# Leaf results of the last tree scattered to token order, in a Macaron block with hard-routed trees

## The chip, the cores and the metric

The kernel runs on one core of a Trainium2 chip. The metric is the device time of one execution in microseconds (us): the median of three runs. Engines are named as the profile names them: PE (TensorE; PEld its weight loads), DVE (VectorE), ACT (ScalarE), POOL (GpSimd) and SP (SyncE, which here only issues transfers).

## The reference, cut to what matters

```python
def fff(x, nw, nb, w1, b1, w2, b2, act):       # a tree of depth 8 with 256 leaves
    node = 0
    for _ in range(8):                          # hard routing, one leaf per token
        node = 2 * node + 1 + (x . nw[node] + nb[node] > 0)
    leaf = node - 255
    h = act(x @ w1[leaf] + b1[leaf])            # 256 -> 16
    return h @ w2[leaf] + b2[leaf]              # 16 -> 256

def ffn(x):
    xn = (x - mean(x)) / sqrt(std(x) + 1e-5)
    q, k, v = fff(xn, q.., relu), fff(xn, k.., relu), fff(xn, v.., relu)
    y = xn + softmax(q k^T / sqrt(256)) v       # one head, 1024 x 1024 per batch
    return y + fff(y, f.., gelu)

x = x + 0.5 * ffn(layernorm(x))
x = x + attention(layernorm(x))   # 16 heads of 16, latent k and v, RoPE, mask causal by pages of 64
x = x + 0.5 * ffn(layernorm(x))
```

x is 4 x 1024 x 256 in float32: 4096 tokens. The two FFNs have the same weights. The layer norm inside an FFN and its own norm are merged into one scale per token.

## The kernel before, in words

**Tiling.** Tokens go in 32 tiles of 128 (NT; a token's row lies on one partition), in groups of 4 tiles (GT), 8 tiles to a batch (TPB). `xres` holds the residual stream in SBUF, `xn` the normed rows, later y, with a column for the leaf number on either side.

**A tree** has five steps. *Route* (`route`, L293): transposes, matmuls with all node weights, comparisons (`bits`, L319), one-hot leaves (`hot`, L332). *Place* (`place`, L438, with `counts`, `ranks`): the 256 leaves are 32 blocks of 8; tokens are sorted by block into groups of 128 slots, each group of one block, so that a group may end in pads. *Scatter* (`scatter`, L506): POOL sends each tile's rows (257 wide, with the leaf number) to their slots in a DRAM buffer `xs`, one indirect DMA per tile. *Leaves* (`leaves`, L590): for each group an `xg` load, transposes (`xgT`), matmul with the block's w1 (`w_..`, turned by `load_first`, L543, from `raw_..` loads), a mask that keeps the token's own leaf (`hm`, L630), transposition with the activation (`hid`), matmul with w2, and the result row `og`, written to a DRAM buffer `os_..` in slot order. 48 groups are fixed; up to 15 more stand in branches (`spare_leaves`), of which the second FFN runs 5 for q and f. *Fetch* (`fetch`, L664, `fetch_b2`, L676): for each tile a POOL gather of the 128 result rows by slot, and one of the b2 rows by leaf, 128 KB each.

Pads must hold no stray leaf number, so `clear` (L240) writes zeros into both `xs` buffers (8.3 MB each) and into the spare parts of `os_q`, `os_k` and `os_v` (2.0 MB each), once, at the head of the first FFN. The clear of `xs[0]` is issued on SP, the rest on ACT.

**An FFN** runs: routes q; building w1 of q; scatter q; routes k beside it; leaves q; routes v; leaves k; leaves v, with gathers for the attention of batch 0; then the attention over 32 query tiles. Each tile has `score` (two matmuls with a width of 512 and a depth of 256 in two parts, maximum `mx` on DVE, exponential `pr` on ACT) and `weigh` (8 transposes, 8 matmuls with `vb`, row `xn` on DVE); one tile is scored ahead of the one weighed. In between stand the gathers of the next batch and the routing of f, four tiles after their last `weigh`. Tree f is placed in two runs: `place_early` for the first 24 tiles during the last batch's attention, with their 24 scatters, and `place_late` for the last 8 after the last `weigh`. Then come 8 scatters, the leaves of f, and in them `settle`, which gathers b2 of f for all tiles and adds y and b2, by halves, to `xres` (L1002). After the last leaf, 32 gathers `y_f` (L668) and 32 additions (L1012) close the FFN; the first FFN takes the moments of each row there, the second writes each tile out.

**Between the FFNs** stands the 16-head attention (MLA below), whose score matmuls (L1155, L1189) fill PE; its first tiles need all moments (`rstd`, L1097).

**The order.** A scheduler orders the instructions of each engine from the program's order and its own estimates; each engine, and each issuing queue, then runs strictly in that order. A tile buffer comes free when its last reader is done, so the number of buffers (`bufs`) sets how far loads run ahead.

Of the kernel before, what the change touches and what calls it, by code (L numbers as in the profile page):

```python
# [24 lines left out]
P = 128  # L25
# [46 lines left out]
def macaron_kernel(ctx: ExitStack, tc: tile.TileContext, a: dict, out: bass.AP):  # L72
# [33 lines left out]
    def sm(shape):  # L106
        return bank("sm", shape)
# [121 lines left out]
    xs = [dram.tile([NSLOT, XW], F32, name=f"xs_{n}") for n in range(2)] * 2  # L229
    osrt = [dram.tile([NSLOT, E], F32, name=f"os_{nm}") for nm in FFFS[:3]]  # L230
    osrt.append(osrt[0])
# [5 lines left out]
    zero = const.tile([P, XW], F32, name="zero")  # L237
    nc.vector.memset(zero, 0.0)
# [42 lines left out]

    def x_of(t):
        return xn[:, t, 1 : 1 + E]

    def row_of(f, t):
        lo = 1 - f % 2
        return xn[:, t, lo : lo + XW]
# [5 lines left out]
    def route(pool, f, t, oh, acc, leaf):  # L293
# [3 lines left out]
        xT = pool.tile([P, KC, GTOK], F32, name="xT", tag="xT")  # L297
        for i in range(0, GT, 2):
            pt = sm([P, KC, 2 * P])
            for k in range(2):  # L300
                for c in range(KC):
                    nc.tensor.transpose(  # L302
                        pt[:, c, k * P : (k + 1) * P], x_of(t + i + k)[:, c * P : (c + 1) * P], ident
                    )
            nc.scalar.copy(xT[:, :, i * P : (i + 2) * P], pt)  # L305
        yield
        bits = pool.tile([P, 2, GTOK], BF16, name="bits", tag="bits")
        for r in range(2):
            pl = sm([P, GTOK])
# [11 lines left out]
        hot = pool.tile([P, 2, GTOK], BF16, name="hot", tag="hot")  # L321
        for lc in range(2):
            ps = sm([P, GTOK])
# [10 lines left out]
        pr = sm([P, GT, NBLK + 2])  # L334
        for i in range(GT):
# [8 lines left out]
        nc.vector.tensor_copy(oh[:, t : t + GT, :], pr[:, :, :NBLK])  # L344
        for i in range(t, t + GT):
            nc.vector.tensor_tensor(acc[:, i + 1], acc[:, i], oh[:, i], ALU.add)
        nc.vector.tensor_copy(leaf[:, t : t + GT], pr[:, :, NBLK])
        lc = leaf_col(f)
        nc.vector.tensor_copy(xn[:, t : t + GT, lc : lc + 1], pr[:, :, NBLK + 1 :])
# [41 lines left out]
    def ranks(pool, oh, acc, slot, lo, hi, first, second=None):  # L391
# [7 lines left out]
        if second:  # L399
            past = pool.tile([P, n, NBLK], F32, name="past", tag="past")  # L400
            nc.vector.tensor_tensor(past, pr, bc(second[0], 1, n), ALU.is_ge)
            nc.vector.tensor_tensor(past, past, bc(second[1], 1, n), ALU.mult)
            nc.vector.tensor_tensor(row, pr, past, ALU.add)
            nc.vector.tensor_tensor(row, row, bc(first, 1, n), ALU.add)
        else:
            nc.vector.tensor_tensor(row, pr, bc(first, 1, n), ALU.add)
# [47 lines left out]
    EARLY = NT - TPB  # L454

    def place_early(pool, oh, acc, slot):

        ng = tiles_of(pool, counts(pool, acc, EARLY), EARLY)
        end = ends_of(pool, "gend", ng, 0.0)
        first = first_row(pool, end, ng)  # L460
        full = pool.tile([P, NBLK], F32, name="full", tag="full")
        nc.vector.tensor_scalar_mul(full, ng, float(P))
        yield
        for lo in range(0, EARLY, NT // 2):
            ranks(pool, oh, acc, slot, lo, min(lo + NT // 2, EARLY), first)
            yield
        gb = pool.tile([P, GCOL], F32, name="gb", tag="gb")
        for h in range(2):
            ended(pool, gb, end, h)
            yield  # L470

        past = pool.tile([P, GCOL], F32, name="gb_past", tag="gb_past")
        nc.vector.tensor_scalar(
            past, cst[:, C_G : C_G + GCOL], end[:, NBLK - 1 :], -float(NBLK), ALU.is_ge, ALU.mult
        )
        nc.vector.tensor_add(gb, gb, past)
        return end, first, full, gb

    def place_late(pool, oh, acc, slot, gblk, sel, end, first, full, gb):


        cnt = counts(pool, acc, NT)
        nc.vector.tensor_sub(cnt, cnt, full)
        ng = tiles_of(pool, cnt, TPB)
        more = ends_of(pool, "gend2", ng, end[:, NBLK - 1 :])

        skip = pool.tile([P, NBLK], F32, name="skip", tag="skip")
        nc.vector.tensor_sub(skip, more, ng)
        nc.vector.tensor_scalar_mul(skip, skip, float(P))
        nc.vector.tensor_sub(skip, skip, first)  # L490
        nc.vector.tensor_sub(skip, skip, full)
        yield
        ranks(pool, oh, acc, slot, EARLY, NT, first, (full, skip))
        yield
        gb2 = pool.tile([P, GCOL], F32, name="gb2", tag="gb2")
        for h in range(2):
            ended(pool, gb2, more, h)
        nc.vector.tensor_add(gb, gb, gb2)
        tile_blocks(gb, more, gblk, sel)
# [43 lines left out]
    def load_first(pool, f, w1, b1p, b1, raws):  # L543


        nc.vector.tensor_copy(b1p, b1)
        for k in range(1, 3):
            for q in range(k, 3):
                one = slice(q * NBLK, (q + 1) * NBLK)
                nc.vector.tensor_sub(b1[one], b1[one], b1p[one])  # L550
                nc.vector.tensor_copy(b1p[one], b1[one])
        nb_half = P // EPB
        for k, (hf, c) in enumerate(PART):
# [4 lines left out]
            for l0 in range(0, LW, 4):  # L558
# [4 lines left out]
                if l0 % 8:  # L563
# [10 lines left out]
    def spare_leaves(*what):  # L574
# [4 lines left out]
            engines=[getattr(mybir.EngineType, e) for e in ("PE", "DVE", "Activation", "SP")],  # L579
# [10 lines left out]
    def leaves(pool, f, w1, w2, b1p, sel, gblk, func, lo=0, hi=SPARE[0]):  # L590
# [3 lines left out]
        blk = {}  # L594
# [791 lines left out]
```

## Time and profile before

| | us |
|---|---|
| median of three runs (lowest to highest) | 3035.63 (3020.66 to 3035.7) |
| the profiled execution | 3026.19 |
| its span | 3024.0 |
| PE busy | 2507.0 (83%) |
| DVE busy | 1508.0 (50%) |
| ACT busy | 1055.0 (35%) |
| POOL busy | 827.2 (27%) |
| first FFN: routes q end, leaves q start, leaves q end | 73.9, 182.2, 269.7 |
| first FFN: attention begins, last weighing, first masked group and last result of f | 541, 913.3, 974.2, 1058.6 |
| MLA's first large matmul | 1121.1 |
| second FFN: routes q end, leaves q start | 2029, 2086 |
| second FFN: attention begins, last weighing, first masked group and last result of f | 2440, 2814.2, 2864.4, 2971.8 |

The mean granted clock of PE was 0.911. DMA moved 309 MB at 102 GB/s over the span, unevenly: near nothing during the MLA, near its most at the head. An engine's busy share over the whole span says little here, since stages with full PE alternate with stages in which it waits; what counts is what each wait is for.

### The profile page before, as it was taken

How to read it: one execution, taken by the hardware profiler on the slowest of the kernel's cores; microseconds unless marked ns; L12 is line 12 of the kernel's file. 1: busy time of each engine (PE TensorE's matmuls, PEld its weight loads, DVE VectorE, ACT ScalarE, POOL GpSimd, SP SyncE). 2: the span in 40 equal slices, each digit the busy share in tenths (PEclk: the TensorE clock that was granted, in tenths of full speed). 3: DMA queues.
4: the chain of work that ended last, by engine and by line, in shares of the span. 5: the costliest groups of instructions: out<-in, count | busy, mean ns of one | idle time of the engine just before them, and what ended most of it. 6: DMA issues, size and time to landing. Idle time of an engine off the chain costs nothing. (4 is left out here: it accounts for less than half of the span.)

```text
span 3024.0 us, 42420 instructions
## 1 busy us (share of the span) xinstructions
PE 2507.0 (83%) x14320; PEld 1506.8 (50%) x14360; DVE 1508.0 (50%) x3993; ACT 1055.0 (35%) x2466; POOL 827.2 (27%) x941
## 2 busy tenths in 40 slices
PE   7398988589893929999999999988889968889492
PEld 3156567356662614444444344355656745566361
DVE  8353544233345456666666576376354533334552
ACT  3134334122221303555555555433334422222130
POOL 0430324644225052100101100005204454431514
PEclk9699889799996959999999999998989889999796
DMA  9936467322114520000000000034546842210454
GB/s 267 296 118 218 150 203 215 123 63 65 42 49 148 162 74 1 1 1 1 1 1 1 1 1 2 1 102 163 174 160 214 245 149 65 69 49 34 145 172 143
DMA packets 225217, 309.26 MB, mean 102 GB/s; under 512 B 28248, under 2 KB 196312, under 8 KB 220888
## 3 DMA queue, kind: packets, MB, share of 16 engines
q1 hardware_dynamic: 148352, 166.10, 17.7%
q0 software_dynamic: 36864, 100.84, 10.8%
q10 hardware_dynamic: 39768, 39.36, 4.3%
q8 instruction: 128, 2.10, 0.3%
q14 instruction: 105, 0.86, 0.1%
HBM read 193.54 MB, written 112.66 MB: 101 GB/s over the span
## 5 line engine op out<-in xcount | busy, mean ns | idle before, releaser
L1162 DVE TENSOR_REDUCE mxh<-big 128x1 f32<-128x512 f32 (+3 forms) x768 | 393.1, 552 | 221.7 <-PE big L1155 219.6
L1196 ACT ACTIVATE pTh<-big 128x512 f32<-128x512 f32 (+3 forms) x768 | 336.8, 491 | 332.5 <-PE big L1155 296.3
L1155 PE MATMUL big<-kTh,qTh 32*128 32x512 f32 (+3 forms) x1536 | 407.8, 534 | 3.2 <-ACT kTh L1137 1.6
L1189 PE MATMUL big<-qTh,kTh 32*128 32x512 f32 (+3 forms) x1536 | 351.9, 529 | 0.0
L722 PE MATMUL sm<-vb,pT 128*128 128x256 f32 x1024 | 259.2, 410 | 64.7 <-DVE mx L703 49.5
L311 PE MATMUL sm<-xT,nwT 128*128 128x512 f32 x512 | 243.5, 620 | 54.4 <-ACT xT L305 54.2
L630 DVE SCALAR_TENSOR_TENSOR hm<-eid,xg,sm 128x128 f32<-128x128 f32 x399 | 138.4, 347 | 299.1 <-PE sm L625 294.7
L639 ACT ACTIVATE hid<-sm 128x128 f32<-128x128 f32 x399 | 110.8, 278 | 491.2 <-PE sm L637 490.3
L722 PEld LDWEIGHTS sm<-vb,pT 128*128 128x128 f32 x1024 | 205.6, 206 | 140.5 <-DVE mx L703 50.3
L694 PE MATMUL two<-kT,qT 128*128 128x512 f32 x512 | 247.9, 608 | 1.3 <-ACTq L584 1.3
L604 PE MATMUL sm<-ident,xg 128*128 128x128 f32 x798 | 166.0, 292 | 60.9 <-DMA xg<-xs 60.9
L1189 PEld LDWEIGHTS big<-qTh,kTh 32*128 32x128 f32 x1536 | 117.6, 183 | 149.2 <-DVE mxh L1162 75.6
L319 DVE TENSOR_SCALAR bits<-sm,thr 128x512 bf16<-128x512 f32 x128 | 95.7, 749 | 184.1 <-PE sm L311 183.8
L311 PEld LDWEIGHTS sm<-xT,nwT 128*128 128x128 f32 x512 | 96.8, 198 | 167.3 <-issue 95.0
L606 DVE COPY xgT<-sm 128x256 f32<-128x256 f32 x399 | 166.9, 418 | 25.4 <-PE sm L604 23.7
L1155 PEld LDWEIGHTS big<-kTh,qTh 32*128 32x128 f32 x1536 | 151.8, 183 | 45.1 <-ACT pTh L1196 27.4
L1207 PE MATMUL sm<-pTh,vpad 128*32 128x512 f32 (+3 forms) x1536 | 166.7, 498 | 4.7 <-ACT pTh L1196 4.7
L646 ACT COPY og<-sm 128x256 f32<-128x256 f32 x399 | 148.6, 372 | 49.1 <-PE sm L644 19.7
L305 ACT COPY xT<-sm 128x512 f32<-128x512 f32 x128 | 69.3, 590 | 191.1 <-PE sm L302 190.9
L508 POOL DMA_INDIRECT xs<-xn,slot_v x64 | 63.4, 991 | 251.9 <-DVE slot_v L412 232.9
L694 PEld LDWEIGHTS two<-kT,qT 128*128 128x128 f32 x512 | 91.3, 195 | 73.7 <-issue 66.9
L508 POOL DMA_INDIRECT xs<-xn,slot_f x64 | 67.7, 1058 | 217.0 <-DVE slot_f L412 198.7
(294 smaller groups left out, 4367.0 us busy)
## 6 DMA issues: line engine op xcount, KB each, us to landing
xg<-xs SPq DMA_DIRECT2D x399, 128.5 KB
os_q<-og SPq DMA_DIRECT2D x202, 128.0 KB
os_v<-og SPq DMA_DIRECT2D x101, 128.0 KB
os_k<-og SPq DMA_DIRECT2D x96, 128.0 KB
raw_q<-in_q_w SPq DMA_DIRECT2D x8, 1024.0 KB
w_q<-in_q_w SPq DMA_DIRECT2D x2, 4096.0 KB
raw_k<-in_k_w SPq DMA_DIRECT2D x8, 1024.0 KB
w_k<-in_k_w ACTq DMA_DIRECT2D x2, 4096.0 KB
```

Source lines behind the costliest of these rows:

```text
L311: nc.tensor.matmul(pl, nwT[:, c, f, r * P : (r + 1) * P], xT[:, c, :], start=(c == 0), stop=(c == KC - 1),)
L604: nc.tensor.transpose(pa[:, c, :], xg[:, x0 + c * P : x0 + (c + 1) * P], ident)
L606: nc.vector.tensor_copy(xT, pa)
L630: nc.vector.scalar_tensor_tensor(hm, eid, xg[:, lf : lf + 1], ph, ALU.is_equal, ALU.mult)
L646: nc.scalar.copy(og, po)
L694: nc.tensor.matmul(ps[:, n0 : n0 + 512], qT[:, c, i * P : (i + 1) * P], kT[:, c, n0 : n0 + 512], start=(c == 0), stop=(c == KC - 1),)
L722: nc.tensor.matmul(po, pT[:, j, :], vb[:, j, :], start=(j == 0), stop=(j == TPB - 1))
L1155: nc.tensor.matmul(ps[:, :n], qT[r : r + HPAD, hg, i * P : (i + 1) * P], kT[r : r + HPAD, hg, n0 : n0 + n], start=True, stop=True,)
L1162: nc.vector.tensor_reduce(maxima(b, hg)[:, i, c, u : u + 1], ps[:, :n], AX.X, ALU.max)
L1189: nc.tensor.matmul(ps[:, off:], kT[r : r + HPAD, hg, j * P : (j + 1) * P], qT[r : r + HPAD, hg, qb * QN + off : (qb + 1) * QN], start=True ...
L1196: nc.scalar.activation(pT[:, u, off:], ps[:, off:], AF.Exp, scale=1.0 / math.sqrt(HD))
L1207: nc.tensor.matmul(acc[r : r + HPAD, off:], vpads[b % 2][:, j, 4 * hg + 2 * pair + u, :], pTs[pair][:, u, off:], start=(j == 0), stop=(j = ...
```

## The change

Five things change.

1. The results of f are scattered by token. A token column (the tile's first token plus the partition) travels with each row of f through a buffer of its own, `xs_f`, 258 wide; its pads hold a number of 4096 or more. In `leaves`, f copies the column to an integer tile `tok` (6 buffers) and POOL scatters `og` to `ytok`, a DRAM buffer in token order; the bounds check skips the pads. So `y_f` is read back as eight plain loads of four tiles (`arrive`). In the first FFN these and the moments are woven into the MLA's start, after a first part for batch 0; in the second they stand before eight writes of the output.
2. `settle` (b2 of f and y added to `xres`) moves into the attention for 28 tiles, two gathers in flight; the last four tiles remain in leaves f.
3. f is placed in three runs, tiles 0 to 23, 24 to 27 and 28 to 31; the last routing is of one tile, the one before of three. w1 of f is copied by ACT alone.
4. Four query tiles are scored before the first is weighed (two of them use buffers of the routing).
5. All clears go to SP, those of the `os` buffers each to a place of its own; `xs_f` is cleared in each FFN, after the loads of f's first weights are asked for.

In the changed program's order on SP in the first FFN: `xs[1]`'s clear, `raw_q` parts 3 and 4, `os_q`'s clear, six `xg` loads of q with a `raw_k` load among them, `os_k`'s clear, three `b_v` loads, `os_v`'s clear, a `raw_k` load, `xs_f`'s clear, the seventh `xg`.

```diff
-    xs = [dram.tile([NSLOT, XW], F32, name=f"xs_{n}") for n in range(2)] * 2
+    xs = [dram.tile([NSLOT, XW], F32, name=f"xs_{n}") for n in range(2)]
     osrt = [dram.tile([NSLOT, E], F32, name=f"os_{nm}") for nm in FFFS[:3]]
-    osrt.append(osrt[0])
+
+    xs += [xs[0], dram.tile([NSLOT, XW + 1], F32, name="xs_f")]
+    ytok = dram.tile([NTOK, E], F32, name="ytok")
...
-    zero = const.tile([P, XW], F32, name="zero")
-    nc.vector.memset(zero, 0.0)
+    zero = const.tile([P, XW + 1], F32, name="zero")
+    nc.vector.memset(zero[:, :XW], 0.0)
+    nc.vector.tensor_scalar_add(zero[:, XW:], pid, float(NTOK))
...
+    RUNS = (0, NT - TPB, NT - GT, NT)
...
+            if f == 3:
+                tok[g] = pool.tile([P, 1], I32, name="tok", tag="tok", bufs=6)
+                nc.vector.tensor_copy(tok[g], xg[:, XW:])
...
+            if f == 3:
+                nc.gpsimd.indirect_dma_start(
+                    out=places[g],
+                    out_offset=bass.IndirectOffsetOnAxis(ap=tok.pop(g), axis=0),
+                    in_=og,
+                    in_offset=None,
+                    bounds_check=NTOK - 1,
+                    oob_is_err=False,
+                )
+            else:
+                nc.sync.dma_start(osrt[f][g * P : (g + 1) * P, :], og)
...
-                            nc.vector.tensor_scalar_mul(zero, count, 0.0)
-                            clear(nc.scalar, xs[1])
-                            for o in osrt[:3]:
-                                clear(nc.scalar, o[SPARE[0] * P :])
...
+                        if first:
+                            for rows in (xs[1], osrt[0][SPARE[0] * P :]):
+                                clear(nc.sync, rows)
...
+                        if first:
+                            clear(nc.sync, osrt[1][SPARE[0] * P :])
...
+                    if first:
+                        clear(nc.sync, osrt[2][SPARE[0] * P :])
...
+            clear(nc.sync, xs[3])
...
+                def settle(t):
+
+                    b2 = fetch_b2(pf, 3, t, leaf[3], bufs=2)
+                    yield
+                    for add in (x_of(t), b2):
+                        nc.vector.scalar_tensor_tensor(
+                            xres[:, t, :], add, 0.5, xres[:, t, :], ALU.mult, ALU.add
+                        )
...
+                        to = rp.tile([P, T], F32, name="pr", tag="xT") if s in (2, 3) else None
+                        scored.append((s, vb, *score(ap, qT, kT, i, to)))
+                        if s == 0:
+                            drain(values)
                         if b or i > 1:
                             next(ahead, None)
-                        elif i:
-                            drain(values)
-                        if late:
-                            t, v, *pr = late
-                            weigh(ap, v, t, *pr)
-                            for path in paths:
-                                for _ in range(1 + (b == B - 1)):
-                                    next(path, None)
-                            if t % GT == GT - 1:
-                                paths.append(route(rp, 3, t - GT + 1, *hot_f, leaf[3]))
-                        late = now
+                        if b and i == 0:
+                            next(ahead, None)
+                        if s >= 3:
+                            while len(scored) > 1:
+                                use()
+                                if s == 3:
+                                    next(ahead, None)
...
+                        if s >= 12:
+                            for t in (s - 12,) if b < B - 1 else (2 * s - 36, 2 * s - 35):
+                                settling.append(settle(t))
+                                next(settling[-1])
+                                if len(settling) > 2:
+                                    drain(settling.pop(0))
...
-                build = load_first(raw, 3, w1, b1p[3], b1, raws)
+                build = load_first(raw, 3, w1, raws, False)
                 w2 = load_second(nc.scalar, wp, 3)
-                for _ in route(rp, 3, t - GT + 1, *hot_f, leaf[3]):
+                for _ in paths[-1]:
                     drain(islice(build, 1))
-                late = place_late(pf, *hot_f, slot[3], gblk[3], sel[3], *placed)
+                late = placing(2)
                 next(late)
-                drain(islice(build, 3))
+                drain(islice(build, 4))
                 next(late)
-                scatter(3, slot[3], views, EARLY)
-                drain(late, build)
+                scatter(3, slot[3], views, RUNS[2])
+                drain(build, late)
+                split_b1(b1p[3], b1)
...
-                what = lp, 3, w1, w2, b1p[3], sel[3], gblk[3], AF.Gelu
-                with_steps(leaves(*what), settle())
+                what = lp, 3, w1, w2, b1p[3], sel[3], gblk[3], AF.Gelu, dram_disjoint_views(ytok, NGRP)
+                steps = leaves(*what)
+                drain(islice(steps, 8))
+                with_steps(steps, *[settle(t) for t in range(NT - GT, NT)])
                 spare_leaves(*what)
-                for t in range(NT):
-                    y = fetch(ep, 3, t, slot[3], bufs=4)
-                    nc.vector.scalar_tensor_tensor(
-                        xres[:, t, :], y, 0.5, xres[:, t, :], ALU.mult, ALU.add
-                    )
-                    if last:
-                        nc.sync.dma_start(
-                            out[t // TPB, (t % TPB) * P : (t % TPB + 1) * P, :], xres[:, t, :]
+
+            if last:
+                with ExitStack() as fs:
+                    ep = stage(fs, "end", 3)
+                    for c in range(NT // GT):
+                        ts_ = slice(c * GT, (c + 1) * GT)
+                        arrive(ep, c, nc.sync)
+                        nc.scalar.dma_start(
+                            out[c * GT // TPB, c * GT % TPB * P : (c * GT % TPB + GT) * P, :].rearrange(
+                                "(i p) e -> p i e", p=P
+                            ),
+                            xres[:, ts_, :],
                         )
-                    else:
-                        rows_moments(ep, moments[0][:, t, :], xres[:, t, :])
+
+    def arrive(pool, c, queue, tag="y", bufs=None):
+
+        ts_ = slice(c * GT, (c + 1) * GT)
+        y = pool.tile([P, GT, E], F32, name="y", tag=tag, bufs=bufs)
+        queue.dma_start(
+            y, ytok[c * GTOK : (c + 1) * GTOK, :].rearrange("(i p) e -> p i e", p=P)
+        )
+        nc.vector.scalar_tensor_tensor(
+            xres[:, ts_, :], y, 0.5, xres[:, ts_, :], ALU.mult, ALU.add
+        )
...
+            def arriving():
+
+                for c in range(NT // GT):
+                    arrive(ap, c, nc.sync if c * GT >= TPB else nc.scalar, "pTh", 5)
+                    yield
+                    for t in range(c * GT, (c + 1) * GT):
+                        rows_moments(ap, mv[:, t, :], xres[:, t, :])
+                        if t % 2:
+                            yield
+
+            come = arriving()
+            for _ in islice(come, 3 * TPB // GT):
+                pass
+            factor(0, TPB)
```

## The prediction

> **What bounds it now.** The page first, its span in 40 slices (75.6 us each): PE is solid except in six places.
>
> ```profile
> PE   7398988589893929999999999988889968889492
> DMA  9936467322114520000000000034546842210454
> ```
>
> Digits 3, 5, 3, 2 and two 4s are the holes: the head of each FFN's first leaves, the passage from attention to leaves f, and the end of each FFN. Then the table of stretches, one for each place that the change touches (the columns after the stretch: its length, busy time of PE, PEld, DVE, ACT and POOL, clock, DMA share, GB/s):
>
> ```profile
> 75.00:182.00 107.00, 54.03 (x276) 31.64 (x278) 38.83 (x98) 24.55 (x39) 30.89 (x32) 0.74 0.74 219
> 541.00:914.00 373.00, 318.33 (x1304) 210.60 (x1312) 135.48 (x323) 88.31 (x167) 159.29 (x168) 0.93 0.23 71
> 914.00:975.00 61.00, 15.84 (x100) 11.83 (x100) 35.24 (x90) 10.95 (x13) 28.85 (x27) 0.65 0.44 145
> 1059.00:1121.00 62.00, 6.69 (x22) 4.31 (x22) 35.00 (x131) 3.58 (x8) 40.20 (x42) 0.55 0.30 89
> 2814.00:2864.00 50.00, 14.80 (x97) 11.01 (x96) 28.56 (x72) 11.30 (x13) 20.95 (x19) 0.69 0.48 159
> 2972.00:3024.00 52.00, 0.00 (x0) 0.00 (x0) 13.61 (x32) 0.00 (x0) 31.69 (x32) 0.51 0.57 167
> ```
>
> Attention is PE's own (318 of 373 us); the rest are waits. For the head, the waits from 60 to 190 us, then ACT's and SP's timelines (start, length, what was issued):
>
> ```profile
> ACT w_q L566 <- DMA os_q<-zero: 56.8, 1, 56.8
> ```
>
> ```profile
> 74.90 34.33 ACTq L242 DMA_DIRECT2D os_q<-zero  x1
> 109.27 11.50 ACTq L242 DMA_DIRECT2D os_k<-zero  x1
> ```
>
> ```profile
> 17.27 28.18 SPq L537 DMA_DIRECT2D b_q<-in_q_b  x3
> ```
>
> An issue right behind an 8.3 MB clear holds its queue until most of the clear has drained: 34.3 us on ACT (xs1), 28.2 on SP (xs0). For the passage, the waits from 2814 to 2880 us (total, times, longest):
>
> ```profile
> POOL xs L508 <- DVE slot_f L412: 25.4, 1, 25.4
> PE sm L604 <- DMA xg<-xs: 24.3, 1, 24.3
> DVE xres L1002 <- DMA b_f<-in_f_b,leaf_f: 20.5, 12, 11.6
> PE sm L622 <- DVE xgT L606: 19.3, 3, 9.2
> ```
>
> PE waits first for slots and scatters, then for DVE, which stands in b2 waits. For the end, the groups from 2972 us:
>
> ```profile
> L668 POOL DMA_INDIRECT y_f<-os_q,slot_f x32 | 31.7, 990 | 95.3 <-SPq L584 84.1 <-DVE xres L1012 4.2 <-DMA y_f<-os_q,slot_f 3.7
> L1012 DVE SCALAR_TENSOR_TENSOR xres<-y_f,xres 128x256 f32<-128x256 f32 x32 | 13.6, 425 | 37.8 <-DMA y_f<-os_q,slot_f 37.8
> ```
>
> 32 gathers at 0.99 + 0.3 us of issue are the tail.
>
> **What the Trainium skill says.** "Trainium Kernel Development and Optimization", Key Constraints: SP's, ACT's and POOL's transfers run on the same 16 engines; another queue saves only issue time. The trace agrees: the clears keep DMA at 0.74 over the head on whichever queue. "DMA: Bandwidth & Descriptors", Queues, rings and completion order: each engine consumes a row in ring order, so loads behind a clear on SP wait for it; the 28.2 us show it. Same page, Anatomy of one DMA: about 2.0 us fixed plus bytes over 436 GB/s, so an estimate of 2.3 us for 128 KB; here POOL's transfers land in 2.7 us in attention and 3.3 to 3.8 beside leaves. The measurement decides.
>
> **The change, part by part.** T is the end of the last weighing (913.3, 2814.2), L the last leaf result (1058.6, 2971.8).
>
> *Head, first FFN.* Leaving ACT free removes up to 56.8 us of waiting; the second FFN, without clears, goes from the end of routes q to leaves q in 57 us where the first takes 108, so about 50 is the most. But in the changed order of SP, xs1's clear stands before raw_q parts 3 and 4. It may start at about 75, and holds them to about 110 (34.3 as on ACT); landing at 114, and the 43 to 47 us that the trace shows from that part's landing to the first leaf of q, gives 158 to 162, not 131. Scatter q still ends near 128. Behind it SP carries six xg loads, os_k's clear, b_v's loads (for which DVE waits in front of routes k's last comparisons, to about 145: +10, so leaves start at about 170), os_v's clear, a raw_k load and xs_f's 8.3 MB, and only then the seventh xg: 15 MB at 300 GB/s is 50 us, so about 182. Group 6 runs then; 42 groups at 1.75 end at 259 against 269.7. **−10** (from +5, where os_q writes fall behind too, to −50). The second clear of xs_f is issued under the MLA, at nothing: DMA is at 0 there; without that cover 28 us.
>
> *Attention.* Four scores ahead: the first weighing waits for values from POOL gathers of 1.25 us whose number doesn't shrink; two score tiles of 3.8 us fill part of it: **−3** each (0 to −10). 28 b2 gathers (35 us POOL) and 56 additions at 0.42 (24 us DVE) stand under PE's 318 of 373 us, POOL at 159 and DVE at 135. DVE is in order and two b_f buffers make it wait; behind it stand mx, for which exp and so PE wait: **+5** (0 to +15). At the end, the last b_f gathers stand on POOL behind 24 scatters (30 us), and DVE's additions ahead of the last pT and xn: **+10** (+3 to +15). Per FFN: **+12**.
>
> *Passage.* Now slots come at T+22.9, first hidden at T+50.2 and T+60.9. In three runs: a one-tile route, then about 28 short DVE operations (8.6 us), slots at T'+21; four scatters (5 us) instead of eight (12.9), xg issued at T'+28, landed and turned at T'+33; the last four b2 waits make it T'+36. All w1 copies on ACT: 16 at 1.03 = 16.5 us under the route, at nothing. The settling of the first 16 groups vanishes, so leaves take 82.5 us for 48 groups, as leaves k does in the second FFN, and 99 for 53 (second FFN's count). Last result at T'+118.5 against T+145.3: **−27**; at T'+135 against T+157.6: **−23** (each ±8); T' = T+12 is charged above.
>
> *Scattered results.* A 0.15 us token copy on DVE, a POOL issue of 1.25 per group: both below 1.545, the steady period now. But the token column has six buffers, and DVE's copy for group g, placed before the masking of g−1, waits until scatter g−6 has landed. From masking to result is 4.23 us; five periods must hold 4.23 plus issue plus landing: with 2.7 landed 1.4 to 1.6, with 3.8 1.6 to 1.8. **+8** over 101 groups (0 to +26).
>
> *Ends.* First FFN: from L to the first large matmul takes 62.5 us. Now: scatter landed at L+4, 4.2 MB at 300 GB/s (six chunks before the first z, 14 us), addition, z at L+24; z to matmul 9.7 as now (1111.4 to 1121.1), two chunks more: L+36. 24 tiles' moments at 0.6 (14 us) mix into the first unit's DVE, of which some 6 us show: **−20** (−12 to −30). The pad memset of 7 us shrinks. Second FFN: 4.2 MB read and 4.2 written at 300 GB/s, 28 us, with landings L+38 instead of L+52: **−14** (−8 to −20).
>
> Sum: −10 + 2×12 − 27 − 23 + 8 − 20 − 14 = **−62**. The profiled execution took 3026.2 us, so 2964; the median is 9.4 higher, the lowest run 5.5 lower, so I put **2967**.
>
> **Rivals.** *Head wholly freed:* the clears hide under routes k; leaves q start near 135. For: only the raw_q position holds them; against: DMA already at 0.74. 40 more: 2927. *Queue and loop cost more:* head nothing, period 1.8 (+26 instead of +8), b_f waits +10 more per FFN: 48 less gain, 3015. For: landings of 3.8 beside leaves q. *Gathers were cover:* the first FFN's end refills with moments and the MLA's loads (0 instead of −20), and the passage stays bound by the slot chain, so that only the settling goes: the first eight groups of leaves f take 21.4 us now, at the steady period 12.4, so −9 per FFN. −10 + 24 − 18 + 8 − 14 = −10: 3019, within half a per cent of before, which is about what runs of this kernel can tell from no change. For: DVE has 35 us of work in the first FFN's end; against: 21.4 us of its waits there are for y_f. *Slower:* the token loop, at leaves f in both FFNs. Without its own term the sum is −70, 0.69 us on each of 101 groups; a period of 1.545 + 0.69 = 2.24 gives five periods of 11.2 us, so 7.0 for issue and landing. Above a landing of some 6.5 us the change loses; at 0.9 per group (landing about 7.5) it is +21: 3056. Against it, 3.8 is the worst median landing in leaves; for it, no trace shows a scatter into token order, and each stands beside xg loads.
>
> **How the numbers follow.** Likeliest 0.53 (own range 2940 to 2992), head freed 0.15, queue and loop 0.17, refilled 0.08, slower 0.07. Faster takes the first three but for 0.02 of the third: 0.83; same 0.09; slower 0.08. The range from 2918 to 3022 leaves out the slower case, and the far half of the second.
>
> **What would show it.** ACT's 56.8 us wait gone; an SP wait at raw_q behind xs1's clear; seventh xg near 180; leaves q ending near 259. DVE waits for b_f before the last pT. First hidden 36 us after the last weighing; leaves f at 1.55 to 1.7 per group, DVE's token copies waiting for ytok if more. First large matmul 42 us after the last scatter's result, end 38. Wrong if SP's clears stall leaves q beyond 185 or ytok landings pass 4.5 us.

## The result and the profile after

The changed kernel takes 3026.97 us (median of 12 runs, 3017.38 to 3033.99), the kernel before 3029.22 beside it; the ratio is 0.9987 (0.9967 to 1.0008): no difference. 2967 was forecast, with a gain of 62 us. The profiled span is 3025.1 us against 3024.0. Four later sets of runs fell on chips on which every kernel takes about 6 to 9% longer; there the comparison comes out otherwise, which the experiments tell below. Until then all numbers are of the first chip. One of the four runs of e4 below was slow (2999.9 us at a granted clock of 0.88, the other three at 0.92 to 0.93), and no time or ratio of e4 counts it.

Where the time went, by stage (us; the marks are the last result of each tree, the last weighing, and in the MLA the first and the last of the score matmuls of L1155, which is L1264 in the changed kernel):

| stage | before | after | difference |
|---|---|---|---|
| start to last result of q | 269.7 | 254.9 | −14.8 |
| to last result of k | 151.1 | 182.2 | **+31.1** |
| to last result of v | 120.3 | 122.2 | +1.9 |
| attention to the last weighing | 372.7 | 404.3 | **+31.6** |
| to last result of f | 144.8 | 116.5 | −28.3 |
| to first large matmul | 62.5 | 31.0 | −31.5 |
| these matmuls of the MLA | 805.6 | 811.0 | +5.4 |
| second FFN: to last result of q | 262.0 | 256.9 | −5.1 |
| to last result of k | 149.5 | 180.2 | **+30.7** |
| to last result of v | 101.7 | 100.8 | −0.9 |
| attention to the last weighing | 374.8 | 402.1 | **+27.3** |
| to last result of f | 157.1 | 128.2 | −28.9 |
| to the end | 52.2 | 34.8 | −17.4 |

The page of the changed kernel shows the same in slices. Slice 5 of PE (digit 4, 302 to 378 us) and slice 31 (a 6) are weaker than before; they hold leaves k.

```profile
PE   7589488678897759999999999898886876889774
DMA  9995357422213460000000000035544752221344
```

The table of stretches of the changed kernel (columns as in the prediction):

```profile
75.00:173.00 98.00, 59.01 (x300) 35.49 (x300) 43.83 (x121) 25.82 (x40) 30.85 (x32) 0.78 1.00 297
335.00:376.00 41.00, 8.82 (x52) 6.88 (x52) 3.86 (x13) 2.99 (x11) 30.80 (x33) 0.61 0.41 134
559.00:964.00 405.00, 325.93 (x1314) 215.35 (x1314) 165.51 (x404) 88.86 (x167) 192.92 (x199) 0.89 0.24 73
964.00:1000.00 36.00, 16.72 (x110) 12.94 (x110) 16.12 (x58) 17.98 (x24) 9.06 (x10) 0.76 0.65 205
1080.00:1111.00 31.00, 5.78 (x22) 3.81 (x22) 22.40 (x81) 3.62 (x9) 9.18 (x12) 0.61 0.80 246
2990.00:3025.00 35.00, 0.00 (x0) 0.00 (x0) 9.80 (x8) 0.29 (x1) 2.17 (x3) 0.54 0.71 241
```

The second row is the surprise: 41 us in the middle of leaves k in which PE works 9, DVE 4 and ACT 3, while only POOL is busy. The same stretch of leaves k in the kernel before, beside the same 32 scatters, has PE at work for 39.56 us:

```profile
350.00:391.00 41.00, 39.56 (x253) 29.03 (x252) 17.94 (x55) 16.52 (x51) 30.91 (x33) 0.98 0.84 260
```

The waits of that stretch in the changed kernel name the cause, and DVE's timeline shows it as one instruction (start, length, operation, idle time before it):

```profile
ACT hid L666 <- PE sm L664: 37.0, 5, 33.8
DVE xn L994 <- DMA xs<-xn,slot_v: 32.9, 1, 32.9
PE sm L646 <- DVE xgT L630: 32.2, 1, 32.2
```

```profile
338.95 0.42 DVE L630 COPY xgT<-sm 128x256 f32<-128x256 f32 x1
372.23 0.26 DVE L994 TENSOR_SCALAR xn<-cst 128x32 f32<-128x32 f32 x1 [32.86 <-DMA xs<-xn,slot_v]
372.38 0.34 DVE L654 SCALAR_TENSOR_TENSOR hm<-eid,xg,sm 128x128 f32<-128x128 f32 x1
```

L994 writes the token numbers into a column of `xn`: 0.26 us of work. The scatter of v reads that column (it is v's leaf number there), so the write must wait until the last of v's 32 scatters has read its row. In the program it stands in attention's preparation; the scheduled order has it in leaves k, between the turning of one group and the masking of another; it needs nothing of leaves k. DVE runs in order, so the masking stands behind it, and with the masking PE and ACT, until the scatters are through. The same happens in the second FFN, 31.5 us.

### The profile page after: what moved, and what is told of

Its sections match the earlier page's. It is cut to its first block, busy times and chain, and to the rows that moved or that the text cites. A ratio compares the mean times of both kernels' runs of the same rounds, so it can differ in the third digit from the quotient of the medians.

```text
span 3025.1 us, 42650 instructions
## 1 busy us (share of the span) xinstructions
PE 2516.5 (83%) x14390; PEld 1513.6 (50%) x14390; DVE 1517.4 (50%) x4101; ACT 1070.6 (35%) x2489; POOL 864.2 (29%) x978
## 3 DMA queue, kind: packets, MB, share of 16 engines
q0 software_dynamic: 38640, 100.90, 10.6%
## 5 line engine op out<-in xcount | busy, mean ns | idle before, releaser
L1264 PE MATMUL big<-kTh,qTh 32*128 32x512 f32 (+3 forms) x1536 | 410.5, 537 | 3.0 <-ACT kTh L1246 1.4
L759 PE MATMUL sm<-vb,pT 128*128 128x256 f32 x1024 | 268.0, 421 | 109.1 <-DVE pT L756 67.4
L759 PEld LDWEIGHTS sm<-vb,pT 128*128 128x128 f32 x1024 | 212.6, 212 | 183.1 <-DVE pT L756 74.0
L316 PE MATMUL sm<-xT,nwT 128*128 128x512 f32 (+2 forms) x528 | 242.6, 603 | 5.7 <-ACT xT L310 4.3
L630 DVE COPY xgT<-sm 128x256 f32<-128x256 f32 x399 | 166.9, 418 | 19.4 <-PE sm L628 17.4
L1264 PEld LDWEIGHTS big<-kTh,qTh 32*128 32x128 f32 x1536 | 152.3, 184 | 44.8 <-ACT pTh L1305 27.4
L324 DVE TENSOR_SCALAR bits<-sm,thr 128x512 bf16<-128x512 f32 (+1 forms) x132 | 96.6, 733 | 154.4 <-PE sm L316 153.6
L316 PEld LDWEIGHTS sm<-xT,nwT 128*128 128x128 f32 x528 | 98.0, 196 | 116.9 <-issue 90.3
L310 ACT COPY xT<-sm 128x512 f32<-128x512 f32 (+1 forms) x130 | 69.6, 583 | 212.2 <-PE sm L307 211.9
L705 POOL DMA_INDIRECT y_k<-os_k,slot_k x64 | 61.3, 959 | 278.0 <-PE sm L925 134.1
L646 PE MATMUL sm<-w_k,xgT 128*128 x384 | 73.6, 318 | 73.4 <-DVE xgT L630 69.6
```

What stands on the lines that cost most here:

```text
L316: nc.tensor.matmul(pl, nwT[:, c, f, r * P : (r + 1) * P], xT[:, c, :], start=(c == 0), stop=(c == KC - 1),)
L630: nc.vector.tensor_copy(xT, pa)
L759: nc.tensor.matmul(po, pT[:, j, :], vb[:, j, :], start=(j == 0), stop=(j == TPB - 1))
L1264: nc.tensor.matmul(ps[:, :n], qT[r : r + HPAD, hg, i * P : (i + 1) * P], kT[r : r + HPAD, hg, n0 : n0 + n], start=True, stop=True,)
```

## The experiments

All kernels but e2 are changes to the changed kernel; e2 is a change to the kernel before. Kernels of one set ran on one chip, with runs of the kernel before in between; ratios are to that. The stages are named by the trees: "leaves q" is the stretch of tree q's leaves.

**The column on POOL, and the column alone in the kernel before.** The first takes the instruction out of DVE's order, the second adds it, unused, to the kernel before.

```diff
-                nc.vector.tensor_scalar_add(
+                nc.gpsimd.tensor_scalar_add(
                     xn[:, :, E + 1], cst[:, C_JC : C_JC + NT], pid
                 )
```

> The changed kernel with one instruction moved: the token column of xn is written by POOL, not by DVE. In the changed kernel DVE stands in this instruction for 32.9 and 31.5 us, in the middle of leaves k, until the last row scatter of v has read xn. Theory (column write in DVE's order is the whole gap): both gaps in leaves k close, leaves k takes about 84 us instead of 115, total about 64 us less than the changed kernel: 2960 to 2968, ratio to before about 0.978. Rival 1 (leaves k stops for transfers, DVE's wait is only where it shows): the gap stays and the total stays near 3025. Rival 2 (the time is lost again in attention, where POOL's gathers of v set the start): leaves k gains 64 us, total under 30 us.

> The kernel before with one instruction added: the write of the token column on DVE at the same place in the program, used by nothing. On DVE it stands, as in the changed kernel, between two groups of leaves k. Theory: leaves k stops for 30 to 33 us in both FFNs and the total is 60 to 66 us above before, about 3090, ratio 1.021. Rival (the gap needs the changed kernel's order of transfers): no gap, 3028.

Measured: e1 0.9771 (0.9752 to 0.9789), 2968.2 us against 3038.1; e2 1.0188 (1.0168 to 1.0208), 3095.7 us. In e1, leaves k runs without a stop (327.3 to 406.5 us for the maskings of 48 groups); POOL does the write after its last gather of that stretch, and nobody waits for it:

```profile
380.38 0.95 POOL L717 DMA_INDIRECT b_k<-in_k_b,leaf_k  x1 [0.30 <-issue]
381.46 0.41 POOL L994 TENSOR_SCALAR xn<-cst 128x32 f32<-128x32 f32 x1
413.22 1.03 POOL L705 DMA_INDIRECT y_k<-os_k,slot_k  x1 [31.35 <-SPq L607]
```

In e2 the waits of leaves k hold the same line, with nothing else of the change present:

```profile
DVE xn L938 <- DMA xs<-xn,slot_v: 31.6, 1, 31.6
```

One instruction, twice executed, costs 57.6 us in the kernel before (3095.7 − 3038.1, a little less than the 60 to 66 that were expected), and without it in DVE's order the changed kernel goes from 0.9987 to 0.9771. All rivals fall: the gap needs no other part of the change, and the gain was not lost again in attention.

**One tile scored ahead.**

```diff
-                        to = rp.tile([P, T], F32, name="pr", tag="xT") if s in (2, 3) else None
+                        to = rp.tile([P, T], F32, name="pr", tag="xT") if False else None
...
-                        if s == 0:
+                        if s == 1:
                             drain(values)
...
-                        if s >= 3:
-                            while len(scored) > 1:
-                                use()
-                                if s == 3:
-                                    next(ahead, None)
+                        while len(scored) > 1:
+                            use()
```

> e1 with one query tile scored ahead at the start of attention, as before, instead of four; the two buffers for b2 of v stay. In the changed kernel the first weighing ends 52.8 us after attention begins, against 33.2, and after eight tiles it is 10 us behind. Theory (the copies of pT stand on DVE behind the additions for vb, which wait for gathers, so that four scores only push the first weighing back): first weighing at 35 to 40, total 10 to 20 us under e1 (5 to 10 per FFN). Rival (two buffers for b2 of v and the longer list of gathers make the loss): first weighing no earlier than 48, total within 5 us of e1.

Measured: 0.9708 (0.9688 to 0.9729), 19.4 us under e1, as expected. The first weighing ends 41.3 us after attention begins (35 to 40 were expected), in e1 52.7; attention is 11.0 and 13.7 us shorter. PE's waits at the start of attention, e1 first and then e3:

```profile
PE sm L759 <- DVE pT L756: 17.7, 2, 13.3
```

```profile
PE sm L755 <- ACT pr L743: 10.5, 1, 10.5
PE sm L759 <- DVE mx L740: 10.1, 1, 10.1
PE sm L759 <- DVE vb L960: 5.8, 2, 3.5
```

With four scores ahead, the copy `pT`, which the first weighing needs, stands on DVE behind additions into `vb` that each wait some 2 us for a gather; in e1 PE has turned `pr` at 562.7 and waits until 576 for a copy of 0.68. With one ahead, the weighing follows the additions as they come.

**b2 of f for 24 tiles in attention.** The bound of the loop becomes `12 <= s < 30`, and leaves f settles the last eight tiles.

> e1 with b2 of f added in attention for 24 tiles, not 28, and for the last eight in leaves f. In the changed kernel tile 30 comes 19.5 us after tile 29, against 9.0 before, since DVE waits for b_f gathers of tiles 24 to 27 that stand on POOL behind 24 scatters. Theory: tile 30 comes about 9 us after tile 29, and leaves f loses 0 to 3 us per FFN to four more additions: total 15 to 26 us under e1. Rival (the wait moves: those gathers only meet the scatters of the last tiles and leaves f starts later by as much): total within 5 us of e1.

Measured: 0.9723 (0.9700 to 0.9746), 14.7 us under e1, at the lower edge of the 15 to 26 expected (the expectations of e8 and e18 reckon with 8 to 12 and with 8.5). Tile 30 comes 11.6 us after tile 29, against 19.9 in e1; but the first masked group of f comes 41.9 and 44.1 us after the last weighing, against 36.2 and 36.1: the additions of eight tiles stand ahead of it on DVE. So the rival has about half: of the 12 and 13 us by which attention is shorter, 6 and 8 return before the first masking.

**The other chips.** The next set is of a second chip, on which the kernel before took 3305.8 us; those after it are of a third with 3296.7 us, of the second again (3311.8), and of a fourth with 3308.3. Times are compared only within a set.

> e1 with the clears of xs1 and os_q held back until the first four tiles of k are routed (the zeros they copy are made then), so that on SP the clear stands behind raw_q parts 3 and 4. In the changed kernel PE waits 33.5 us for raw_q behind the clear and leaves q starts at 173. Theory (that position is what keeps the head's gain at 15 instead of some 50 us): the wait for raw_q falls under 8 us, leaves q starts at 145 to 158, total 15 to 28 us under e1. Rival (the head is short of DMA, whose share is 1.00 from 75 to 182 us, so that the wait only moves from raw_q to xg): leaves q starts within 6 us of e1, total within 6 us.

> e1 with 12 buffers for the token column in leaves f instead of 6. In the changed kernel DVE waits 49.6 us in all, in 71 pieces of at most 2.0, for scatters into ytok before it may overwrite one. Theory of the prediction (the loop of 4.23 us plus issue and landing over five periods is close to the period without it): the waits vanish and leaves f gains 0 to 4 us per FFN, total 0 to 8 us under e1. Rival (the waits are on the path in full): 20 us or more.

> e1 with b2 of f added in leaves f for all 32 tiles, as before the change, and none in attention. Theory: attention ends 15 to 20 us earlier per FFN (13 at the last tiles, the rest in between), but the first groups of leaves f stand behind additions again, which costs 10 to 25 us per FFN: total from 20 us under e1 to 10 above. Rival (the b2 gathers in attention cost nothing but the end, and leaves f pays in full): 20 us or more above e1.

> e1, e3, e4 and e5 together: column on POOL, one tile scored ahead, b2 of f for 24 tiles in attention, clears behind raw_q. If the three gains are of different places they add: e1 less 20 (e3), less 8 to 12 (e4), less what e5 gives (15 to 28): 2908 to 2925, ratio to before about 0.96. If the earlier leaves q meet the same transfers, or the earlier attention only waits longer at its end, 2930 to 2945.

The edit of e5 moves the making of the zeros from the end of routes q to the fourth step of routes k; that of e6 is `bufs=12` for `tok`; e7 sets the loop's condition to false and settles all 32 tiles in leaves f. Measured: e5 0.9687 (0.9661 to 0.9713), e6 0.9708 (0.9678 to 0.9738), e7 0.9870 (0.9839 to 0.9901), e8 0.9708 (0.9683 to 0.9733).

e5: the wait for raw_q is gone, but leaves q starts at 165 us (145 to 158 were expected; 173 in e6, which has the clears where e1 has them), and the total is that of e6 within 2 us, nearer to the rival. SP's timeline shows where the wait went (some of its rows):

```profile
115.15 0.38 SPq L245 DMA_DIRECT2D xs<-zero  x1
115.58 31.45 SPq L245 DMA_DIRECT2D os_q<-zero  x1
154.29 3.02 SPq L622 DMA_DIRECT2D xg<-xs  x6
176.28 0.43 SPq L245 DMA_DIRECT2D xs_f<-zero  x1
179.40 31.92 SPq L622 DMA_DIRECT2D xg<-xs  x1
```

The clear of xs1 now holds the next issue 31.5 us, and with it the first xg loads (154 instead of 135 in e6); that of xs_f holds the ninth xg 31.9 us inside leaves q. That second stop costs little here: from first to last masking leaves q takes 116.9 us in e5 and 114.8 in e6, since on this chip leaves q stands in that stretch anyway (below).

e6: leaves f takes 80.5 and 89.5 us (first to last masking) against 81.2 and 91.6 in e5, its neighbour with six buffers: 0.7 and 2.1 us. With twelve buffers the copies wait for their xg load instead (14.8 us in the first FFN). So the token waits, though all over the trace of the changed kernel, were hardly on the path:

```profile
L659 DVE CAST tok<-xg 128x1 int32<-128x1 f32 x42 | 6.4, 153 | 25.2 <-DMA ytok<-og,tok 25.1
```

e7: against e6, attention is 10.6 and 13.5 us shorter, the way from the last weighing to the last result of f 41.3 and 38.0 us longer. So the b2 part gives about 27 us per FFN on this chip. The rival (20 us or more above e1) is right: e7 is 53.5 us above e6, and its own theory, from 20 under e1 to 10 above, priced leaves f (10 to 25) too low.

e8 (3210.8 us) doesn't beat e6 (3204.9): the clear stops leaves q as in e5, and the gains of e3 and e4 are not seen. The next set asks why, with e1 as its base.

> e1 once more, beside the next three on one chip, so that they can be compared with it: ratio to before 0.975 to 0.979, as in its first run, if the chip is alike; as base for the others in any case.

> e5 with one edit more: the clear of xs_f in the first FFN is asked for during attention (its pad numbers are made there), so that it no longer stands on SP among the xg loads of leaves q, where in e5 it held the ninth for 31.9 us. Theory (both clears are a cost of position): no stop inside leaves q, leaves q ends 12 to 30 us before e1's. Rival (8.3 MB of xs1 and the 2 MB clears still have to drain before xg): leaves q starts where e1's does, total within 6 us of e1.

> e1 with e3's and e4's edits. The places are different (first and last weighings), so the gains add: 27 to 33 us under e1, ratio to before about 0.968. Rival (an earlier first weighing only lengthens a later wait): under 22 us.

> e11 with e10's edit: 12 to 30 us under e11 if the head gains, equal if it does not. Ratio to before 0.958 to 0.968.

e10's further edit makes the pad numbers after the tenth score, and asks for the first clear of xs_f only then. Measured: e9 0.9673 (0.9644 to 0.9702), e10 0.9632 (0.9602 to 0.9662), e11 0.9715 (0.9687 to 0.9743), e12 0.9695 (0.9662 to 0.9728). e9, which is e1 again, comes out lower than on the first chip (0.975 to 0.979 was expected). In e10 leaves q runs without the stop behind xs_f's clear and ends at 281.2 against 291.3: −10.1 us, below the 12 to 30 expected; the intervals overlap. e12 is 4.8 us under e11, where 12 to 30 were expected. e11 is not faster than e9 but 15 us slower, so the gains of e3 and e4 together don't carry to this chip. For e4 the trace shows why: tile 30 comes 18.3 us after tile 29 in e9 and in e11, for DVE has the same waits at the end of attention in both, and not those for b2:

```profile
DVE xn L760 <- remote: 10.5, 1, 10.5
DVE mx L739 <- remote: 7.9, 1, 7.9
```

"remote" says that DVE was released by something that the trace doesn't hold. These waits lie beside the scatters of f. In e1 on the first chip DVE has neither of them there, but one of 9.1 us for a b2 gather.

> The changed kernel itself, beside the next three. On a chip like that of its first runs: ratio 0.997 to 1.001, with DVE's wait of some 32 us for the column in leaves k. On a chip like that of e9, where leaves k stands for some 35 us beside the scatters of v anyway: the column's wait lies partly in that stretch and costs less, so the ratio is nearer to e9's 0.967, 0.97 to 0.985.

> e3 once more. Theory (the order at the start of attention): ratio 0.969 to 0.973 on a chip like that of e3, first weighing near 41 us after attention begins. On a chip like that of e9 the ratio may be lower, as e1's was; the first weighing comes at least 8 us earlier than in e13 on any chip.

> e14 with all of b2 of f added in leaves f, as before the change; two buffers for b2 of v. Theory (buffers): first weighing 40 to 42 us after attention begins, as in e3; attention (to the last weighing) 378 to 383 us, against 372.7 in the kernel before; leaves f longer than e14's by 25 us or more per FFN. Rival (the b2 gathers of f make the first weighing late): 33 to 35 us.

> e15 with three buffers for b2 of v, as before the change. Theory (buffers): first weighing 33 to 36 us after attention begins and attention 371 to 375 us, so 8 us per FFN under e15. Rival (the list of gathers, or the later start of the POOL queue): no earlier than e15's, total within 4 us.

Measured, on the chip of e5 to e8 again: e13, the changed kernel itself, 0.9691 (0.9656 to 0.9727); e14 0.9699 (0.9665 to 0.9733); e15 0.9816 (0.9779 to 0.9852); e16 0.9838 (0.9806 to 0.9870). So on this chip the change is faster by 3.1%, a little more than was expected of it even here (0.97 to 0.985), and e14, with the column on POOL and one tile scored ahead, is no faster. DVE's waits in leaves k, e13 first and then e14, with PE's of e14:

```profile
DVE xn L994 <- DMA xs<-xn,slot_v: 21.1, 1, 21.1
DVE hm L654 <- remote: 10.5, 2, 7.4
```

```profile
DVE hm L654 <- remote: 33.2, 3, 19.2
PE sm L646 <- DVE xgT L630: 30.2, 5, 15.3
```

With the column DVE stands 21.1 + 10.5 us, without it 33.2: leaves k, from the first masking to the last result, takes 122.0 us in e13 and 121.6 in e14. So the column's wait costs nothing here beside a stall that is there without it. That stall is DVE's. In leaves k of e9 (third chip) the masking at 407.9 us reads a product that PE had finished at 393.6, and three before it are 1 to 6 us late; in e1 on the first chip every masking beside the scatters starts within 0.1 us of the time when its product and DVE are ready. PE follows: where e9 and e13 call PE's wait at L646 "issue", it ends within 0.1 us of the turning (`xgT`) that L646 reads. It is so in each of the stretches in which 32 scatters run beside leaves: from first to last masking, leaves q and k take 114.3, 118.6, 129.6 and 119.8 us in e9 against 80.8, 79.2, 96.5 and 79.4 in e1. The scatters themselves take no longer (32 in some 41 us on both chips). Of the 209 us by which the profiled e9 is longer than e1, 170 lie in the two FFNs' stages up to the last results of q and k, 39 in attention; the MLA's matmuls take 801.8 and 803.6. What holds DVE is open. By an estimate from the ratios, the column, 2.2% of the time on the first chip (0.9987 − 0.9771), would account for most of the difference between 0.9987 and 0.9691; the kernel before has no profile of these chips, so that isn't shown.

e14: the first weighing comes 6.2 us earlier than in e13 in both FFNs (not 8), but attention is no shorter (433.3 against 433.5, 437.4 against 427.1). e15 has an attention of 417.8 and 420.5 us, where 378 to 383 was expected from the first chip's times, and the way from there to the last result of f is 40 and 37 us longer than in e14 (25 or more was expected). From e15 to e16 the third buffer brings the first weighing from 54.6 and 58.7 to 48.0 and 48.3 us after attention begins (40 to 42 and 33 to 36 were expected), but attention to its end changes by +1.6 and −6.0, and the total by nothing that the intervals show. The buffers do move the first weighing; that they make attention shorter is not shown.

> e10 once more. Theory (position of the clears): PE's wait of 33.5 us for raw_q is gone, and leaves q ends at least 10 us before the 260.3 of e1; ratio to before 0.966 to 0.974 on a chip like that of e1 (0.977 there without it), 0.96 to 0.967 on one like that of e9. Rival: the clear only moves its cost to xg, leaves q ends within 4 us of 260.3 (or of 291.3 on a chip like that of e9).

> e11 once more. On a chip like that of e1: gains of e3 (19.4) and e4 (8.5) add, ratio 0.966 to 0.970. On one like that of e9: 0.969 to 0.974, as in e11, so no better than e1 there.

Measured on a fourth chip (before: 3308.3): e17 0.9624 (0.9591 to 0.9658), e18 0.9704 (0.9668 to 0.9741). Leaves q ends at 283.7 in e17 and at 293.6 in e18, which has the clears where the change put them: −9.9, as on the third chip. e18 repeats e11.

The versions that beat both kernels: on the first chip e1 (0.9771) and e3 (0.9708); on the third and fourth e10 and e17, which are the same kernel, have the lowest ratios (0.9632, 0.9624), with e9's interval reaching into that of e10.

## Why the prediction was wrong

**The step that failed** is "Scattered results". It priced what the token column costs in leaves f (0.15 us per copy, 1.25 us of POOL, the loop over six buffers) and left out the write that fills the column in `xn`: three lines of the whole diff, which are not among those printed ahead of the prediction. It put this write at nothing, without a reason. In the traces it is 32.9 + 31.5 = 64.4 us of the changed kernel on this chip, and e1 and e2 show that it is the cause. −62 and +64.4 make +2.4; the profiled spans differ by +1.1. For b_f and for `tok` the prediction asked what stands behind a wait on its engine; for this line it did not.

That the rest of the sum comes out is luck: attention costs 58.9 us in the two FFNs where 24 were put, 35 more, and all other stages but those of k gain 119.6 where 86 were put, 34 more. Term by term:

- **Head, −10:** measured −14.8. The mechanism is as put: PE waits for raw_q behind the clear, and the seventh xg comes behind that of xs_f at 173.75 (182 was put).

```profile
PE sm L581 <- DMA raw_q<-in_q_w: 33.5, 1, 33.5
```

```profile
76.48 0.39 SPq L245 DMA_DIRECT2D xs<-zero  x1
82.35 23.34 SPq L548 DMA_DIRECT2D raw_q<-in_q_w  x2
148.96 1.25 SPq L245 DMA_DIRECT2D xs_f<-zero  x1
173.75 7.12 SPq L622 DMA_DIRECT2D xg<-xs  x3
```

  DVE's wait for b_v was 4.9 us, not 10. The DMA share of 0.74 that the prediction reads as holding "on whichever queue" had the clears of that stretch on ACT alone; with them on SP it is 1.00 from 75 to 173 us. The rival "head wholly freed" is not reached as far as the clears were moved: e10 and e17 end leaves q 10 us earlier where it put 40 more. There xs1's clear still stands on SP ahead of the first xg and holds the next issue 34.9 us in e10, at a DMA share of 0.86 (75 to 165 us), so that it isn't shown that DMA is the limit.
- **Attention, +12 per FFN:** measured +31.6 and +27.3. The first term had the wrong sign: four scores ahead, put at −3, make attention 11 to 14 us longer (e3). The last b_f waits, put at +10, show as tile 30 coming 19.5 us after tile 29 against 9.0, and without the last four of them attention is 12 to 13 us shorter (e4); DVE's waits there:

```profile
DVE xres L987 <- DMA b_f<-in_f_b,leaf_f: 19.5, 5, 8.8
```

  The rest, some 1 to 9 us if the two add (no run on this chip has both), is only argued: additions and gathers in between (put at +5) and the first weighing, still 41.3 us after attention's start in e3 against 33.2 before.
- **Passage, first masking at T'+36:** 36.1 and 36.3 us, so the mechanism holds. The "T+50.2" for the kernel before is the first product with w1 in the second FFN (2864.4, also in the table ahead of the prediction); the first masking comes at 2873.9, as late after the last weighing (59.7 us) as in the first FFN. Last result after the last weighing: 116.5 and 128.2 us, put at 118.5 and 135.
- **Token loop, +8:** 0.7 and 2.1 us at most (e6, on the second chip); one period of leaves f, 78.5 us over 47 steps, is 1.67 us, that of leaves k in e1 1.68.
- **Ends, −20 and −14:** −31.5 to the first large matmul, more than the range of −12 to −30, and −17.4. The 6 us put for moments in the MLA's first unit aren't shown: its matmuls take 5.4 us more than before, but 803.6 us in e1, less than before, with the same edit. The second end is eight additions that wait for loads:

```profile
L1109 DVE SCALAR_TENSOR_TENSOR xres<-y,xres 128x1024 f32<-128x1024 f32 x8 | 9.8, 1226 | 22.2 <-DMA y<-ytok 22.2
```

**Rivals and range.** The result, 3027, lies nearest "gathers were cover" (3019), but not by its mechanism: the ends did not refill. It is outside the range (up to 3022) by 5 us. No rival had a wait at a place that the change does not name. Two figures of the rivals don't hold: 3.8 us is not the worst median landing beside leaves (four b_k gathers beside leaves k took 4.6), and 3056 is counted from 3035.6 us, the others from 3029.

## What to carry to other kernels

In these runs a write into a tile that an indirect scatter still read waited for that scatter to land (32.9 and 31.5 us), and since the engine runs in order, everything behind it waited too. So list every new instruction with what it overwrites and who last reads that, and look it up in the scheduled order, not in the program. A repair that worked here is to give the write to the engine that issues the reads and is idle afterwards (e1). An 8.3 MB clear held the next issue on its queue for 23 to 36 us, on SP and on ACT; it cost nothing that shows where nothing on that queue was due (e10, xs_f's clear during attention). And a gain measured on one chip need not be there on the next: a wait can lie in a stall that another chip has anyway.

## What the runs showed of the hardware

- The same two kernels compare as 0.9987 on one chip and 0.9691 on another. On three further chips the stretches with 32 row scatters beside leaves take 33 to 40 us longer: DVE starts some instructions late, one in e9 14 us after its input was there, released by something that the trace doesn't hold. The scatters (0.96 us and 0.30 between) and the MLA are as fast as on the first chip. The cause is open.
- A 0.26 us DVE instruction held three engines for 32.9 us.
- Waits that fill the trace can be off the path: DVE's 25 us of waits for scatters into `ytok` in the first FFN's leaves f give way to waits for xg with twelve token buffers, for a gain of at most 2.1 us.
